# Layer 0 attention of a two-layer kernel: a small total moves to another PSUM bank, and the raw contexts' loads move to another queue and other buffers

## The chip, the cores and the metric

The kernel runs on one core of a Trainium2 chip. The metric is the device time of one execution in microseconds (us). It has five engines that work side by side, each through its own queue in order: TensorE (PE; its weight loads are shown apart as PEld), VectorE (DVE), ScalarE (ACT), GpSimd (POOL) and SyncE (SP), which here only starts transfers. GpSimd can start transfers too. A transfer is started by an instruction of one of these queues and then runs on the core's 16 DMA engines.

## The reference

Two transformer layers run over 8 x 256 tokens of width 512, and both attend to a context of the same shape. Only layer 0's attention matters here, with the weights of the feed-forward part after it, which are prepared meanwhile, and one input of layer 1's attention:

```python
Q = einsum('bshd,hde->bshe', xh, Wh)       # x after its layer norm, 4 heads of 128
K = einsum('bshd,hde->bshe', kh, Wh)       # k = v = context
V = einsum('bshd,hde->bshe', vh, Wh)
scores = einsum('bshe,bthe->bhst', Q, K) / sqrt(hd)
A = maximum(abs((scores * Dn[None]).sum(axis=0)), 1.0)   # summed over the batch
O = einsum('hst,bthe->bshe', A, V).reshape(b, s, dim)
Y = (O - mu) / sqrt(var + GN_EPS) * gn_gamma + gn_beta
return relu(x @ wg_w) * Y @ wo_w
# the feed-forward part's weights:
scale = 1.0 / clip(mean(abs(w)), EPS)
w_q = clip(round(w * scale), -1.0, 1.0) / scale
```

The weights w1, w2, w3 of the feed-forward part become ternary, so each needs the mean of its absolute values first. Layer 1's attention uses the context as its values and ends each head with a normalisation; the kernel takes the mean of each head of 32 off the raw context beforehand and writes the result to device memory.

## The kernel before

Tokens are cut into 16 tiles of 128 (P); a chunk is 512 tokens (CH), so four chunks hold two batch items each. The code of `layer0_attention` is written as loops in Python, but the instructions' order on each queue is not the text's: a planner takes all instructions with their dependencies, an estimated duration for each and the text's order as a priority, and lays them out in time. Each queue then runs in exactly that order, and semaphores hold an instruction until its inputs are there and its buffer is free. Tiles are taken from pools by tag: tiles of one tag share a fixed number of buffers (two in the pool `work` unless said otherwise, one in the PSUM pool `ps`), and a new tile waits until the last use of the buffer's earlier tile is over.

The stage runs as follows.

1. SP loads the residual x, the transposed context `ctxT`, the weights and the decay table `dec`.
2. A loop over the tiles n takes the layer norm (`stats`, `normed`) and transposes it; `queries` (L282) makes one product `pq` for each chunk c and head h, which VectorE copies to a tile q of tag "wy" (L286); `scores` (L289) multiplies q with the context and sums over all chunks in four PSUM tiles. Sixteen pairs (c, h) follow each other. From n = 6 on, each step also calls `ternary.add`: a piece of a weight (up to 768 KB) is loaded by SP into a tile `wst` (L156, two buffers) and ScalarE adds up its absolute values (L166) in `part`.
3. The sums are multiplied with the decay table; Abs and max follow (L323 to L325).
4. A loop over the 16 tiles i: `attended` (L340) makes the output `po` with the values, its layer norm y on VectorE and ScalarE (L71 to L78), and two GpSimd passes over y (L354, L355); `centered` (L327) loads a raw context tile (tag "raw"), takes each head's mean on VectorE (L334, L335), subtracts it on GpSimd (L336), sets each head's last column to one (L337) and stores the tile to `vc_d` (L338). `gated` multiplies with the gate's product `pw` (L360, wy), `turned` transposes wy on TensorE into the PSUM tag "t" (line 108 in the profile, a helper) and ScalarE copies it (L365), and `output` multiplies with `wo` (L371, pz) and adds to x (L372). In every odd i the `values` of a later batch item follow: TensorE makes `pv` (PSUM tag "pv"), ScalarE copies it (L255).
5. Each i ends with `ternary.round`: a weight piece is loaded again, scaled by ScalarE (L191), clipped by VectorE (L192), and a step later written as bf16 (L182). Ahead of the first piece of each weight, `scale` (L168) has TensorE add `part` over the partitions into the PSUM tile wtot, which VectorE reads (L173) and turns into the weight's scale.

`centered` depends on nothing else of the stage, so the planner places it well ahead of its place in the text.

Of the kernel before, what the change touches and what calls it, by code (L numbers as in the profile page):

```python
# [19 lines left out]
F32 = mybir.dt.float32  # L20
# [10 lines left out]
P = 128  # L31
D = 512
KD = D // P
# [4 lines left out]
CH = 512  # L38
NCH = T // CH
H0 = 4  # L40
# [91 lines left out]
class TernaryWeights:  # L132
# [34 lines left out]

    def scale(self, n):  # L168
        nc, g = self.g.nc, self.g
        tot = self.ps.tile([P, KD], F32, tag="t", name="wtot", bufs=1)  # L170
        nc.tensor.matmul(tot, lhsT=g.ones[:, :P], rhs=self.part[:, n], start=True, stop=True)
        mean = g.small.tile([P, 1], F32, tag="wmean", name="wmean")
        nc.vector.tensor_reduce(mean, tot, AX.X, ALU.add)  # L173
        nc.vector.tensor_scalar(mean, mean, 1.0 / (D * FF), 1e-5, ALU.mult, ALU.max)
        nc.vector.reciprocal(self.sc[n], mean)
        nc.vector.reciprocal(g.iw[:, n : n + 1], self.sc[n])
# [19 lines left out]
def layer0_attention(g, tc, cp, qpool):  # L196


    nc = g.nc
# [4 lines left out]
    with ExitStack() as ctx:  # L204
        wp = ctx.enter_context(tc.tile_pool(name="a0w", bufs=1, reuse_waits="tile"))
        work = ctx.enter_context(tc.tile_pool(name="a0work", bufs=2, reuse_waits="tile"))
# [6 lines left out]
        for c in range(NCH):  # L213
            for i in range(c * CH // P, (c + 1) * CH // P):
                nc.sync.dma_start(out=g.X[i], in_=g.x[i * P : (i + 1) * P, :])
            nc.sync.dma_start(
                out=g.ctxT[c],
                in_=g.ctxT_d[:, c * CH : (c + 1) * CH].rearrange("(k p) t -> p k t", p=P),
# [49 lines left out]
        def stats(i):  # L268
            mv = g.small.tile([P, 2], F32, tag="mv", name="mv")
            norm_stats(g, mv, g.X[i])  # L270
            sd = g.small.tile([P, 1], F32, tag="sd", name="sd")
            nc.scalar.activation(sd, mv[:, 1:2], AF.Sqrt, bias=g.eps["ln"])
            return mv, sd
# [8 lines left out]
        def queries(c, h):  # L282
            pq = ps.tile([P, CH], F32, tag="pq", name="pq", bufs=2)
            nc.tensor.matmul(pq, lhsT=G[:, h, :], rhs=xnT[c][:, h, :], start=True, stop=True)
            q = work.tile([P, CH], F32, tag="wy", name="q")
            nc.vector.tensor_copy(q, pq)  # L286
            return q

# [9 lines left out]
        of, q = {0: stats(0)}, {}  # L298
        for n in range(NT + H0 + 1):
            if n + 1 < NT:  # L300
                of[n + 1] = stats(n + 1)
            if n < NT:
                normed(n, *of.pop(n))
            if 0 <= n - H0 < NT:
                q[n - H0] = queries(*divmod(n - H0, H0))
            if 0 <= n - H0 - 1:
                scores(*divmod(n - H0 - 1, H0), q.pop(n - H0 - 1))
            if n < 4:
                values(*divmod(n, 2))
            elif n >= 6:  # L310
                ternary.add()
# [15 lines left out]
        def centered(i):  # L327


            raw = work.tile([P, D], F32, tag="raw", name="raw")  # L330
            nc.sync.dma_start(out=raw, in_=g.ctx[i * P : (i + 1) * P, :])
            by_head = raw.rearrange("p (h d) -> p h d", d=HD1)
            mean = g.small.tile([P, H1], F32, tag="mean", name="mean")
            nc.vector.tensor_reduce(mean, by_head, AX.X, ALU.add)  # L334
            nc.vector.tensor_scalar(mean, mean, 1.0 / HD1, None, ALU.mult)  # L335
            nc.gpsimd.tensor_sub(by_head, by_head, mean.unsqueeze(2).to_broadcast([P, H1, HD1]))  # L336
            nc.gpsimd.memset(by_head[:, :, HD1 - 1 :], 1.0)  # L337
            nc.gpsimd.dma_start(out=g.vc_d[i * P : (i + 1) * P, :], in_=raw)  # L338
# [37 lines left out]
        wy = {}  # L376
        for i in range(NT + 1):
            if i < NT:
                y = attended(i)
                centered(i)  # L380
            if i:
                wyT = turned(wy.pop(i - 1))
            if i < NT:
                wy[i] = gated(pw, y)
            if i + 1 < NT:
                pw = gate(i + 1)
            if i:
                output(i - 1, wyT)
            if NT - 2 <= i < NT:
                g.begun.append(ffn_turned(g, *ffn_input(g, work, i - NT + 2)))  # L390
            if i % 2 and i // 2 + 2 < B:
                for j in range(2):
                    values(i // 2 + 2, j)
            ternary.round()
# [280 lines left out]
def layer1_attention(g, tc, gates):  # L675
    nc = g.nc
    with ExitStack() as ctx:
# [19 lines left out]
        with tc.tile_pool(name="a1ps2", bufs=1, space=PSUM, reuse_waits="tile") as ps, tc.tile_pool(name="a1work", bufs=2, reuse_waits="tile") as work:  # L697
# [112 lines left out]
            def attended(b, hid, rs):  # L810

                nc.gpsimd.tensor_mul(flat(hid), flat(hid), rs.unsqueeze(2).to_broadcast(shape))  # L812
                for j in range(2):
                    i = 2 * b + j
                    hj = hid[:, j, :, :HD1]
                    x, scale = (t.rearrange("p (h d) -> p h d", d=HD1) for t in (g.X[i], lns))
                    nc.gpsimd.tensor_mul(hj, hj, scale)
                    nc.gpsimd.tensor_add(x, x, hj)
# [704 lines left out]
```

## Time and profile before

| what | us |
|---|---|
| median of 3 runs | 1121.75 |
| lowest and highest of them | 1116.63, 1122.53 |
| the profiled execution's own time | 1119.75 |
| its span in the profile | 1118.0 |
| first raw load issued (SP) | 27.5 |
| last raw store issued (GpSimd) | 144.0 |
| last output product pz begins | 242.4 |

The profile comes from one execution. Its rows give a start, a duration, the engine, the line in the kernel, and the operation as output<-inputs; a bracket at the end gives the time that the engine had stood idle before it, and the instruction or transfer whose end released it. In tables of waits the columns are the total, the number of times and the longest. The name of an engine with a q (SPq, POOLq) is its queue, where transfers are started. A wait for several things is put down to the one that came last.

### The profile page before, as it was taken

The page shows a single profiled execution, that of the slowest core. Times are in us where ns is not written, and L with a number is a line of the kernel's source. Part 1 is how long each engine was busy: PE and PEld are TensorE (multiplying, and loading weights), DVE is VectorE, ACT ScalarE, POOL GpSimd, SP SyncE. Part 2 cuts the span into 40 slices and gives each one's busy share as a digit, 9 for nine tenths or more (in the row PEclk, how much of TensorE's full clock was granted, in tenths as well). Part 3 has the DMA queues.
Part 4 walks back from the last instruction along what each step waited for, and adds up shares of the span by engine and source line. Part 5 has one row for each costly group of instructions (what it writes and reads, how often), then busy time and mean ns, then how long its engine had stood idle before and what let it go on. Part 6 is the DMA issues. An engine that isn't in the chain of part 4 may idle for free.

```text
span 1118.0 us, 14714 instructions
## 1 busy us (share of the span) xinstructions
PE 1018.8 (91%) x5207; PEld 614.9 (55%) x5222; DVE 540.5 (48%) x1443; ACT 411.8 (37%) x701; POOL 374.6 (34%) x347
## 2 busy tenths in 40 slices
PE   6979699988899958899889899999999999999994
PEld 5745465543344435555544344555666666777782
DVE  6545445468888755998872883121222111222120
ACT  4345245135576636578752101111212222211211
POOL 0134432230000100254562204454444555544422
PEclk9989899999999989899999999999999999999997
DMA  9676331012233211212012326786777878889982
GB/s 341 249 263 210 128 118 47 1 38 54 54 62 63 44 48 43 67 61 75 24 56 104 93 107 189 172 209 180 205 198 182 215 217 220 223 225 242 236 200 36
DMA packets 100483, 153.65 MB, mean 137 GB/s; under 512 B 38600, under 2 KB 41288, under 8 KB 100376
## 3 DMA queue, kind: packets, MB, share of 16 engines
q1 hardware_dynamic: 81488, 106.94, 31.2%
q0 software_dynamic: 18672, 45.58, 18.1%
q8 instruction: 43, 0.70, 0.3%
q14 instruction: 40, 0.33, 0.1%
q10 hardware_dynamic: 240, 0.10, 0.0%
HBM read 111.24 MB, written 33.49 MB: 129 GB/s over the span
## 4 chain that ended last, share of the span: by engine, by line
PE 68%; DVE 9%; DMA 9%; ACT 7%; issue 3%; POOL 2%; SPq 0%; POOLq 0%; DVEq 0%; ACTq 0%
PE po L1272 13%; PE pg L1255 12%; PE pu L1255 12%; PE p L556 4%; PE pz L371 3%; PE pw L316 3%; PE pt L1312 3%; DMA hqT<-hq 2%; DMA vc_d<-raw 2%; DMA raw<-in_ctx 2%; ACT xe L731 1%; PE pqk L746 1%; PE po L969 1%; DVE ct L754 1%; PE pv L250 1%
## 5 line engine op out<-in xcount | busy, mean ns | idle before, releaser
L1260 DVE TENSOR_TENSOR act<-pu,sg 128x288 f32<-128x288 f32 (+8 forms) x68 | 32.4, 476 | 317.0 <-PE pu L1255 317.0
L1297 POOL DMA_INDIRECT xg<-h_d,tok_of x84 | 81.3, 968 | 205.5 <-DVE of L1307 69.3
L1316 POOL DMA_INDIRECT out_x<-eo,to x84 | 129.8, 1545 | 57.4 <-ACT eo L1354 36.1
L1272 PE MATMUL po<-w,act 128*128 128x512 f32 (+3 forms) x448 | 141.1, 492 | 0.0
L1255 PE MATMUL pg<-xT,w 128*128 128x288 f32 (+7 forms) x512 | 138.4, 413 | 0.8 <-issue 0.8
L1255 PE MATMUL pu<-xT,w 128*128 128x288 f32 (+7 forms) x512 | 136.7, 410 | 0.0
L1354 ACT ACTIVATE eo<-po,slotw 128x512 f32<-128x512 f32 (+3 forms) x112 | 64.2, 578 | 173.2 <-PE po L1272 169.4
L1255 PEld LDWEIGHTS pu<-xT,w 128*128 128x128 f32 x512 | 97.2, 190 | 29.1 <-issue 3.0
L1255 PEld LDWEIGHTS pg<-xT,w 128*128 128x128 f32 x512 | 93.6, 190 | 35.0 <-issue 15.5
L1259 ACT ACTIVATE sg<-pg 128x288 f32<-128x288 f32 (+8 forms) x68 | 28.9, 425 | 213.2 <-PE pg L1255 213.2
L1272 PEld LDWEIGHTS po<-w,act 128*128 128x128 f32 (+3 forms) x448 | 54.4, 161 | 56.1 <-issue 46.3
L556 PE MATMUL p<-wq,xqT 128*128 128x512 bf16 (+1 forms) x379 | 79.5, 361 | 3.1 <-DMA xqT<-xq 2.1
L754 DVE SCALAR_TENSOR_TENSOR ct<-pqk,xe 128x768 f32<-128x768 f32 x64 | 58.3, 950 | 23.7 <-ACT xe L731 11.8
L1313 DVE COPY xT<-pt 128x512 f32<-128x512 f32 (+3 forms) x84 | 51.9, 618 | 20.7 <-PE pt L1312 20.7
L316 PE MATMUL pw<-wg,xnT 128*128 128x512 f32 x128 | 61.1, 623 | 0.0
L556 PEld LDWEIGHTS <-xqT 128*128 128x128 bf16 x384 | 36.7, 98 | 44.2 <-DMA xqT<-xq 6.4
L371 PE MATMUL pz<-wo,wyT 128*128 128x512 f32 x128 | 57.9, 595 | 3.0 <-ACT wyT L365 3.0
L731 ACT ACTIVATE xe<-pd 128x512 f32<-128x512 f32 x96 | 53.9, 598 | 4.7 <-PE pd L727 4.3
L1312 PEld LDWEIGHTS pt<-ident,xg 128*128 128x128 f32 (+4 forms) x336 | 38.9, 140 | 24.4 <-PE po L1272 11.1
L100 DVE BATCH_NORM_STATS2 st<-x 128x6 f32<-128x512 f32 x64 | 43.8, 685 | 12.3 <-DMA x<-in_x 6.0
L812 POOL TENSOR_TENSOR hid<-hid,rsq 128x1024 f32<-128x1024 f32 x8 | 15.3, 1913 | 102.2 <-PE pqk L750 76.3
L575 PE MATMUL py<-wq,hqT 128*128 128x512 bf16 x168 | 41.2, 380 | 8.1 <-DMA hqT<-hq 7.6
(287 smaller groups left out, 1676.3 us busy)
## 6 DMA issues: line engine op xcount, KB each, us to landing
w<-in_w SPq DMA_DIRECT2D x32, 1024.0 KB
w<-in_w SPq DMA_DIRECT2D x32, 512.0 KB
wst<-in_w1T SPq DMA_DIRECT2D x8, 704.0 KB
wst<-in_w3T SPq DMA_DIRECT2D x8, 704.0 KB
wst<-in_w2T SPq DMA_DIRECT2D x6, 768.0 KB
x<-in_x SPq DMA_DIRECT2D x16, 256.0 KB
ctxT<-in_ctxT_d SPq DMA_DIRECT2D x4, 1024.0 KB
raw<-in_ctx SPq DMA_DIRECT2D x16, 256.0 KB
```

The lines of the kernel that those rows point to most:

```text
L316: nc.tensor.matmul(pw, lhsT=xnT[c][:, k, o : o + P], rhs=wg[:, k, :], start=k == 0, stop=k == KD - 1)
L371: nc.tensor.matmul(pz, lhsT=wyT[:, k, :], rhs=wo[:, k, :], start=k == 0, stop=k == KD - 1)
L556: nc.tensor.matmul(pp[:, : z - a], lhsT=xqT[:, k, :], rhs=w[:, k, a:z], start=k == 0, stop=k == KD - 1)
L731: nc.scalar.activation(out, pd, AF.Exp)
L754: nc.vector.scalar_tensor_tensor(ct[:, r : r + 2, :], pqk[:, :, : S + P], 1.0 / math.sqrt(HD1), xe[:, r : r + 2, :], ALU.mult, ALU.mult,)
L1255: nc.tensor.matmul(pp[:, :n], lhsT=w[:, k, cols], rhs=xT[:, k, :n], start=k == 0, stop=k == KD - 1)
L1272: nc.tensor.matmul(po[h * n : (h + 1) * n, :cols], lhsT=act[:, m, j * P : j * P + n], rhs=w[:, m, h * cols : (h + 1) * cols], start=m == 0 ...
L1297: nc.gpsimd.indirect_dma_start(out=xg[:n], out_offset=None, in_=h_d, in_offset=bass.IndirectOffsetOnAxis(ap=g.tok_of[:n, r, j : j + 1], ax ...
L1312: nc.tensor.transpose(pt[:, k, :n], xg[:n, k * P : (k + 1) * P], g.ident[:n, :n])
L1313: nc.vector.tensor_copy(xT, pt[:, :, :n])
L1316: return nc.gpsimd.indirect_dma_start(out=g.out, out_offset=bass.IndirectOffsetOnAxis(ap=rows, axis=0), in_=eo, in_offset=None, compute_op ...
L1354: nc.scalar.activation(eo[:n, at : at + cols], po, AF.Copy, scale=w[r][:n, j : j + 1])
```

## The change

Three lines change. The total wtot of the weights' sums takes a buffer of the PSUM tag "pv" (one bank, that of the values) instead of one of tag "t" (one bank, that of the transposes). The queries of the last chunk's heads 2 and 3 take buffers of tag "raw" instead of "wy". The raw contexts are loaded by GpSimd's queue instead of SP's. As raw tiles and these two queries now share two buffers, the first raw tiles can be loaded only when the last scores have read those queries. The number of buffers, the data and all arithmetic stay.

```diff
     def scale(self, n):
         nc, g = self.g.nc, self.g
-        tot = self.ps.tile([P, KD], F32, tag="t", name="wtot", bufs=1)
+        tot = self.ps.tile([P, D], F32, tag="pv", name="wtot", bufs=1)[:, :KD]
...
             pq = ps.tile([P, CH], F32, tag="pq", name="pq", bufs=2)
             nc.tensor.matmul(pq, lhsT=G[:, h, :], rhs=xnT[c][:, h, :], start=True, stop=True)
-            q = work.tile([P, CH], F32, tag="wy", name="q")
+
+            last = c == NCH - 1 and h >= H0 - 2
+            q = work.tile([P, CH], F32, tag="raw" if last else "wy", name="q")
             nc.vector.tensor_copy(q, pq)
...
             raw = work.tile([P, D], F32, tag="raw", name="raw")
-            nc.sync.dma_start(out=raw, in_=g.ctx[i * P : (i + 1) * P, :])
+            nc.gpsimd.dma_start(out=raw, in_=g.ctx[i * P : (i + 1) * P, :])
```

## The prediction

> **What bounds the kernel now.** I read the page first (which engine fills the span), then the busy time by stretch (where that engine is not full), then the waits of the stage that the change touches, then the order of instructions on each queue around the longest waits.
>
> ```profile
> span 1118.0 us, 14714 instructions
> PE 1018.8 (91%) x5207; PEld 614.9 (55%) x5222; DVE 540.5 (48%) x1443; ACT 411.8 (37%) x701; POOL 374.6 (34%) x347
> ```
>
> TensorE fills 91% of the span, so a saving counts only where TensorE stands idle. The stretches of layer 0 attention show where (columns: stretch, its length, busy time of each engine with instruction counts, granted TensorE clock, share of DMA, GB/s):
>
> ```profile
> 58.00:63.00 5.00, 3.18 (x15) 2.17 (x14) 2.78 (x6) 2.33 (x4) 1.60 (x3) 1.00 0.93 296
> 63.00:80.00 17.00, 11.98 (x57) 7.84 (x57) 7.46 (x18) 8.65 (x14) 6.55 (x10) 0.92 0.70 238
> 80.00:147.00 67.00, 55.77 (x226) 33.34 (x225) 33.89 (x75) 28.45 (x34) 32.83 (x43) 0.89 0.55 185
> 147.00:187.00 40.00, 40.00 (x178) 24.70 (x178) 20.91 (x40) 15.86 (x20) 10.71 (x8) 1.00 0.22 70
> ```
>
> From 147 us on TensorE is full at full clock: by then the last raw context has been centered (last load issued at 134.5 us, last store at 144.0). Before 147 it loses time, and these waits name the losers (58 to 247 us):
>
> ```profile
> PE pt L108 <- DVE wmean L173: 8.2, 1, 8.2
> PE pt L108 <- DVE wmean L174: 5.0, 1, 5.0
> PE pz L371 <- ACT wyT L365: 3.0, 3, 1.7
> PE pt L108 <- DVE wy L360: 2.1, 3, 1.1
> PE s L293 <- DVE q L286: 1.8, 1, 1.8
> PE pv L250 <- ACT v L255: 0.4, 1, 0.4
> ```
>
> Together 20.5 us; 2.5 of them lie after 235 us, at the stage's end, where the change has no part. So 18.0 us of waits remain, and behind the two long ones the next two gate tiles run slowly: 5.41 and 5.31 us where such eight matmuls take 3.60 at full clock, 1.8 + 1.7 = 3.5 us. In all 21.5 us, under 2% of the run, can be had here.
>
> Now the longest wait, TensorE's lines and then VectorE's of the same moment:
>
> ```profile
> 125.74 0.39 PE L351 MATMUL po<-v,dec 128*128 128x128 f32 x2
> 134.28 1.11 PE L108 MATMUL pt<-ident,wy 128*128 128x128 f32 x4 [8.15 <-DVE wmean L173]
> 135.19 5.31 PE L316 MATMUL pw<-wg,xnT 128*128 128x512 f32 x8
> ```
> ```profile
> 129.09 0.69 DVE L360 SCALAR_TENSOR_TENSOR wy<-pw,y 128x512 f32<-128x512 f32 x1 [3.63 <-POOL y L355]
> 129.69 0.68 DVE L334 TENSOR_REDUCE mean<-raw 128x16 f32<-128x512 f32 x1
> ...
> 132.67 0.69 DVE L334 TENSOR_REDUCE mean<-raw 128x16 f32<-128x512 f32 x1 [2.09 <-DMA raw<-in_ctx]
> 133.39 0.17 DVE L335 TENSOR_SCALAR mean<-mean 128x16 f32<-128x16 f32 x1
> 133.47 0.68 DVE L372 TENSOR_TENSOR x<-pz,x 128x512 f32<-128x512 f32 x1
> 134.08 0.15 DVE L173 TENSOR_REDUCE wmean<-wtot 128x1 f32<-128x4 f32 x1
> ```
>
> The transposes' input wy was ready at 129.78 (129.09 + 0.69); their PSUM bank was not, because wtot lay in it and its reader L173 stood in VectorE's queue behind a mean that waited for a raw context. So the chain is: store of a raw tile lands late, its buffer's next load starts late, VectorE's in-order queue holds on L334, and everything behind it (wtot's reader, bn_stats, the new queries) is late.
>
> **The change, part by part** (against the profiled execution, 1119.75 us with a span of 1118.0; it lies 2.0 us under the median of the three runs, 1121.75, from which I forecast).
>
> *The total's bank.* No instruction is added or removed. The transposes (tag t) no longer wait for L173/L174. At the first wait this is worth nothing: wy L360 ends at 78.72 + 0.69 = 79.41, the transposes start at 79.47. At the second they could start at 129.8 instead of 134.28, 4.5 us; if ScalarE's order stayed, the copy wyT (136.98, behind a ScalarE activation that waits for the same VectorE queue) would still hold the output matmuls to 137.6 instead of 140.3, which leaves 2.7. At most the whole stall with its slow clock goes: 8.15 + 1.71 = 9.9. Bounds 2.7 and 9.9. I take 7.9: all but one VectorE wait for a raw context of mean size, 17.5 us / 9 = 1.94 us (the row of L334 on the raw load), which stays exposed. The new wait, values (L250) for the total's reader, I cost at nothing: totals run at 72, 124 and 175 us, the next values' matmuls at 89, 144 and 184, nine us later at the least; without that cover it would cost what the bank costs now.
>
> *The last two queries in raw's buffers.* The first raw load can now start only when a query buffer is released, after the scores at about 61 us, instead of at 27.5. The 1.8 us wait of the scores (query copy L286 at 59.80, behind mean L334 that waited 2.91 us for its load) must go: no mean can be in front of a query any more. Saved: 1.8. What moves: in the trace five raw tiles were centered before the first y (POOL 48 to 72 us). Five loads, five stores, five times 0.69 + 0.17 us on VectorE and 1.05 + 0.12 on POOL go past the query copies, past the table's Abs/max work and into the loop over tiles, on VectorE's and POOL's queues. VectorE is half busy there (33.9 of 67 us), POOL too; so the work fits, but its waits come along. Three iterations that held a pair of raw tiles without the 8 us stall lost 0.42 + 0.54 + 1.66 + 0.46 = 3.1 us, 1.0 each; five tiles are 2.5 iterations more: +2.5 (bounds 0, and 2.5 x 3.4 = 8.5, with 3.4 us what an iteration from 79 to 147 us exceeds the later ones by: transposes at 79.5 and 147.4 us span three iterations with values and two without, 67.9 us, where later ones take 10.9 and 9.1, 50.9 in all; 17 over 5).
> Five loads of 256 KB and about four stores also leave the stretch up to 72 us, where DMA is 70 to 93% busy; 2.3 MB at its 238 to 296 GB/s are 8 to 10 us of transfer. The weights' pieces (ScalarE waited 1.2 to 3.5 us for each) land sooner. This bears on the 5 us wait: po was done at 69.0, but its bn_stats came at 70.48 (behind a mean) and its sd only at 74.63 on ScalarE, behind an Abs that waited 2.64 us for its piece. From there: y 75.14, POOL 76.1 to 78.7, wy 79.4. Bounds: 0, or all 5.0 + 1.8. I take 2.0, one typical piece wait less; the first raw store and load still collide with these pieces.
>
> *The loads on POOL's queue.* SP loses 16 issues of 0.33 us and their waits for stores, 42.3 us in all:
>
> ```profile
> SPq L331 <- DMA vc_d<-raw: 42.3, 12, 8.2
> ```
>
> Behind them only weight pieces were queued, which ScalarE mostly had to release anyway; worth nothing more than the 2.0 above. POOL gains 16 issues. Nearest rows are its own direct transfers of the same size, 562 ns an issue (9 us in all, beside its 72.5 us of waiting for y), and for landing:
>
> ```profile
> L338 POOL DMA_DIRECT2D vc_d<-raw x16: 557/562/774, 49.9 to 144.0; - x16
> DMA to landing us min/median/max: 2.3/4.5/6.5
> ```
> ```profile
> lns<-in_ln_scale POOLq DMA_DIRECT2D x1, 256.0 KB, 3.4
> ```
>
> A rule speaks against this part. The sixteen POOL issues differ by 0.22 us at most although VectorE worked half the time. The Trainium skill ("SBUF — State Buffer", the "DVE blocks DMA" trap) says that a transfer issued by GpSimd stands still while VectorE runs in a mode that takes both ports, about 3.1 us instead of 0.62, and to use the other queues. By the rule 16 loads are late by 2.5 us each, 40 us of lateness, and as much of it exposed as in the trace (18.0 us of TensorE waits to 17.5 us of L334's waits) would make the change slower by over 25 us. By the row it is at most 0.2 us a load, 3 us, hidden. I follow the row, the same queue beside the same VectorE work.
>
> The new wait: a load waits on POOL for the store that empties its buffer, 4.5 us after issue. Queued behind it are y's multiply and add (L354, L355), for which wy and then the transposes wait. In the trace two stores are followed at once by y (2.6 us). If the loads come after y, only 4.5 - 2.6 = 1.9 us of wait is left, with nothing urgent behind it: cost 0. If they come before, y is late by up to 4.5 us against a slack of 1.9 (wy done 154.6, transposes 156.5) to 3.4 us (173.3, 176.7). I take 0, as y is ready when the stores have been issued; the other end is the second rival.
>
> Sum: -7.9 - 1.8 - 2.0 + 2.5 + 0 = -9.2 us: 1110.6 for the profiled execution, 1112.5 from the median. The next thing to be late is VectorE's mean behind its load, at about 1 us an iteration.
>
> **The rivals.** *First, nothing to measure.* Only the bank's certain part (2.7) and the query wait (1.8) come, and 2.5 goes back: -2.0, 1119.8. For it: L334 still waits for loads on an in-order queue, now in 16 cases in the loop, and the order of all queues is planned anew; against it: the 8 us stall needs the shared bank. *Second, slower: POOL's queue becomes the wait.* Loads stand ahead of y in all eight iterations that take a pair: each makes y late by 4.5 + 0.56 - 2.5 (middle of the slack) = 2.6 us; 8 x 2.6 = 20.6, less the sum's 9.2: +11.4, 1133. It decides from four such iterations (4 x 2.6 > 9.2). For it: y has the tightest path of the loop. Against: POOL waited 72.5 us for y's input, so a load can be placed in that gap. *Third, all of it:* with the means off the queries' way every stall before 147 goes, -21.5: 1100.
>
> **How the numbers follow.** Likeliest case 0.50 (1100 to 1116, third included), nothing to measure 0.23, slower 0.27. About 0.5%, 5.6 us, can be told from no change: faster below 1116.1, slower above 1127.4. Range 1099 to 1130: down to the full recovery, up into the slower rival, of which about half (loads ahead of y in seven or eight iterations) is left out. The likeliest case alone: 1100 to 1116.
>
> **What would show it.** Right: no wait of pt for wmean; no wait of s for q; first raw load after 60 us on POOL's queue; busy TensorE in 80 to 147 us above 60 of 67. Wrong: POOL y L354 or its neighbours waiting for the store vc_d, pt waiting for wy by 2 us or more in many iterations, POOL loads taking far over 3.4 us to land, or a TensorE wait for raw work that runs on past 165 us. A layer 0 stage that ends earlier with no earlier end of the run would refute the claim that a saving here passes through.

## The result

The change made the kernel slower. Over 20 runs of each on the same chip the medians are 1117.26 us before and 1123.43 us after; the ratio of the times is 1.0039, with a 95% interval of 1.0022 to 1.0057. That is 2.5 to 6.4 us more, about 4.4, where 9.2 less had been forecast. The three runs shown before the prediction (1121.75) lay on the high side of this kernel's own spread.

The profiled execution of the changed kernel has the same span as that of the kernel before, 1118.0 us, so one profile of each shows no difference at the end. The stage does. Line numbers are two higher from the queries on: L333 is the raw load, L336/L337 the mean, L338 the subtraction, L340 the store, L356/L357 the passes over y, L362 wy, L367 wyT, L373 the output product. First the page's head, then the busy time by stretch (stretch, length, busy time of PE, PEld, DVE, ACT and POOL with counts, granted clock, DMA share, GB/s).

```profile
span 1118.0 us, 14715 instructions
PE 1027.3 (92%) x5222; PEld 617.5 (55%) x5222; DVE 542.7 (49%) x1443; ACT 412.6 (37%) x701; POOL 385.2 (34%) x363
```
```profile
58.00:63.00 5.00, 5.00 (x23) 3.38 (x22) 1.84 (x4) 3.70 (x7) 1.34 (x2) 1.00 0.74 229
63.00:80.00 17.00, 11.58 (x53) 7.45 (x52) 7.82 (x23) 7.63 (x13) 9.94 (x15) 0.87 0.83 280
80.00:147.00 67.00, 56.00 (x209) 32.59 (x207) 33.78 (x68) 24.52 (x29) 39.51 (x54) 0.88 0.50 168
```

TensorE is now full from 58 to 63 us, where it waited for a query before. From 63 to 147 nothing is better: 67.6 us busy of 84 after, 67.8 before (62.7 and 69.9 in the second profiles further down), and the clock is 0.87 and 0.88 where it was 0.92 and 0.89. The waits of TensorE in the stage (total, times, longest):

```profile
PE pt L108 <- DVE wy L362: 7.2, 4, 3.0
PE pt L108 <- DVE wmean L174: 5.4, 1, 5.4
PE pv L250 <- ACT v L255: 3.6, 2, 3.3
PE pz L373 <- ACT wyT L367: 2.5, 4, 0.7
```

The 8.2 us wait for wmean's L173 and the 1.8 us for q are gone. In their place the transposes wait for wy itself. (The 5.4 us against L174 is such a wait too: L174 ends at 76.52, but wy, which the transposes need and which stands just in front of it, ends at 76.46.) What is new on GpSimd's and VectorE's queues, and VectorE's row of before (L334) last:

```profile
POOL raw L333 <- DMA vc_d<-raw: 16.5, 7, 5.7
```
```profile
DVE mean L336 <- DMA raw<-in_ctx: 26.8, 10, 7.7
```
```profile
DVE mean L334 <- DMA raw<-in_ctx: 17.5, 9, 3.6
```

GpSimd stands 16.5 us on loads whose buffer is still being stored, and VectorE's wait for raw tiles grew from 17.5 to 26.8 us. GpSimd's order of time shows what stands behind such a load:

```profile
80.93 1.28 POOL L356 TENSOR_TENSOR y<-y,gam 128x512 f32<-128x512 f32 x1
83.97 0.56 POOL L333 DMA_DIRECT2D raw<-in_ctx  x1 [1.77 <-DMA vc_d<-raw]
84.55 1.28 POOL L357 TENSOR_TENSOR y<-y,bet 128x512 f32<-128x512 f32 x1
...
106.63 0.54 POOL L333 DMA_DIRECT2D raw<-in_ctx  x1
112.83 0.54 POOL L333 DMA_DIRECT2D raw<-in_ctx  x1 [5.66 <-DMA vc_d<-raw]
115.03 1.04 POOL L338 TENSOR_TENSOR raw<-raw,mean 128x512 f32<-128x512 f32 x1 [1.66 <-DVE mean L337]
116.13 0.13 POOL L339 MEMSET raw<- 128x16 f32 x1
116.55 0.56 POOL L340 DMA_DIRECT2D vc_d<-raw  x1 [0.30 <-POOL raw L339]
117.13 1.27 POOL L356 TENSOR_TENSOR y<-y,gam 128x512 f32<-128x512 f32 x1
```

At 83.97 a load is placed between the two passes over one y (y 1, counted by iterations). At 106.63 the planner put a pair of loads and the work of a raw tile ahead of y 3, whose first pass came at 117.13. GpSimd's queue alone does not explain that: y 3's input was written only at 116.19. VectorE shows why, with the longest of its waits:

```profile
106.23 0.17 DVE L101 BATCH_NORM_AGGREGATE mv<-st 128x2 f32<-128x6 f32 x1
114.05 0.69 DVE L336 TENSOR_REDUCE mean<-raw 128x16 f32<-128x512 f32 x1 [7.65 <-DMA raw<-in_ctx]
114.65 0.17 DVE L73 BATCH_NORM_AGGREGATE mv<-st 128x2 f32<-128x6 f32 x1
...
115.38 0.81 DVE L78 TENSOR_SCALAR y<-po,mv,rs 128x512 f32<-128x512 f32 x1
```

The load of 106.63 took 7.4 us to land, the longest of the sixteen:

```profile
DMA to landing us min/median/max: 2.8/3.5/7.4
```

It ran beside two weight pieces that SP had started at 105.03 (DMA 0.91 busy from 106 to 112 us), and y's own statistics (L73) stood behind its mean. So VectorE's queue held y 3 up for 7.6 us, GpSimd's for another 0.9 (116.19 to 117.13).

The landmark in all that follows is the start of the last output product, the stage's end on TensorE: 242.38 us before, 244.10 after. The same two programs profiled once more give the measure of chance:

> The kernel before, profiled a second time. If the stage's end is set by the order of the queues and not by chance, the last product begins within 1 us of 242.4; the later stages may differ by several us with the granted clock.

> The changed kernel, profiled a second time: last product within 1 us of 244.1 by the same theory. If the 3 us that its first profile lost between 242 and 692 us are chance of the clock, this profile shows another figure there; if they belong to the change, again 2 to 4 us more than before.

The last product's line, of the kernel before again and of the changed kernel again:

```profile
238.71 3.70 PE L371 MATMUL pz<-wo,wyT 128*128 128x512 f32 x8 [0.68 <-ACT wyT L365]
```
```profile
247.71 3.70 PE L373 MATMUL pz<-wo,wyT 128*128 128x512 f32 x8 [0.68 <-ACT wyT L367]
```

The expected 1 us was too narrow: the stage's end moves by 3.6 to 3.7 us between executions of one program. Means are 240.5 before and 245.9 after, 5.4 us later. In the second profile of the changed kernel the longest wait of VectorE stands at the same place, in front of y 3's statistics:

```profile
117.17 0.69 DVE L336 TENSOR_REDUCE mean<-raw 128x16 f32<-128x512 f32 x1 [9.03 <-DMA raw<-in_ctx]
```

### The profile page after: what moved, and what is told of

The parts are those of the page before. It is cut to its first block, busy times and chain, and to the rows that moved or that the text cites. A ratio compares the mean times of both kernels' runs of the same rounds, so it can differ in the third digit from the quotient of the medians.

```text
span 1118.0 us, 14715 instructions
## 1 busy us (share of the span) xinstructions
PE 1027.3 (92%) x5222; PEld 617.5 (55%) x5222; DVE 542.7 (49%) x1443; ACT 412.6 (37%) x701; POOL 385.2 (34%) x363
## 4 chain that ended last, share of the span: by engine, by line
PE 68%; DVE 10%; DMA 8%; ACT 7%; POOL 4%; issue 3%; SPq 0%; POOLq 0%; DVEq 0%; ACTq 0%
PE po L1274 13%; PE pg L1257 12%; PE pu L1257 12%; PE p L558 3%; PE pz L373 3%; PE pt L1314 3%; DMA raw<-in_ctx 3%; PE pw L318 2%; DMA hqT<-hq 2%; ACT xe L733 1%; PE pqk L748 1%; PE s L295 1%; PE pq L284 1%; DMA vc_d<-raw 1%; PE po L971 1%
## 5 line engine op out<-in xcount | busy, mean ns | idle before, releaser
L318 PE MATMUL pw<-wg,xnT 128*128 128x512 f32 x128 | 63.6, 643 | 0.0
L373 PE MATMUL pz<-wo,wyT 128*128 128x512 f32 x128 | 58.1, 597 | 2.6 <-ACT wyT L367 2.5
```

Of the source, the lines that this page charges most:

```text
L318: nc.tensor.matmul(pw, lhsT=xnT[c][:, k, o : o + P], rhs=wg[:, k, :], start=k == 0, stop=k == KD - 1)
L373: nc.tensor.matmul(pz, lhsT=wyT[:, k, :], rhs=wo[:, k, :], start=k == 0, stop=k == KD - 1)
```

## The experiments

All edits are to the kernel before unless another is named; "time" is the ratio to the kernel before, with its interval.

| kernel | last product, us | median, us | time |
|---|---|---|---|
| before (two profiles) | 242.4, 238.7 | 1117.26 | 1 |
| bank alone | 237.7 | 1119.24 | 0.998 (0.9957 to 1.0003) |
| queries alone | 237.5 | 1120.83 | 0.9999 (0.9982 to 1.0015) |
| queue alone | 254.0 | 1133.84 | 1.012 (1.0083 to 1.0157) |
| bank + queries | 236.7 | 1119.12 | 0.998 (0.9958 to 1.0003) |
| queries + queue | 249.0 | 1125.51 | 1.0046 (1.0026 to 1.0066) |
| all three: the change (two profiles) | 244.1, 247.7 | 1123.43 | 1.0039 (1.0022 to 1.0057) |
| the change, y first | 240.3 | 1118.13 | 0.9978 (0.9954 to 1.0002) |
| the change, no means | 250.0 | not comparable | not comparable |
| spread buffers, SP | 228.3 | 1105.91 | 0.9895 (0.9854 to 0.9937) |
| spread buffers, half of the loads on GpSimd | 227.4 | 1108.30 | 0.9906 (0.987 to 0.9941) |
| spread buffers, GpSimd | 229.4 | 1108.49 | 0.9895 (0.9861 to 0.9928) |
| spread buffers, GpSimd, 8 stores too | 230.2 | 1106.03 | 0.9881 (0.984 to 0.9922) |

The groups were run against their own runs of the kernel before (medians 1117.26 to 1121.31), so kernels of different groups are compared by the ratios, not by the medians.

**The three parts one by one.** The diffs are the three hunks of the change, each alone, and the first two together.

> Only the total's PSUM bank is changed. The measure is the start of the last output product pz in the profile (242.4 us before, 244.1 after the whole change) beside the time. If the bank matters as the prediction's first step had it: the 8.2 us wait of the transposes shrinks to 2 to 5 us, the last product begins at 235 to 240, the time falls by 3 to 7 us. If VectorE's late queue was the real cause and the bank only where it showed: the transposes wait for wy or for a later step instead, the last product begins at 241 to 243, the time moves by less than 2 us.

> Only the last two queries take raw's buffers; the loads stay on SP. Theory POOL (the loads on POOL's queue make y late): this part alone gains the 3 us that the scores' end gained in the whole change, last product at 238 to 241. Theory CROWD (all sixteen raw tiles now fall into the loop, whichever queue loads them): the last product at 244 to 250, as late as after the whole change or later, since the shared bank is still there; the time 2 to 8 us up.

> Only the loads' queue is changed; two raw tiles are still loaded early. Theory POOL: loads that wait for stores stand before y on POOL; last product at 245 to 252, time 3 to 10 us up. Theory CROWD: POOL's queue is harmless, last product at 241 to 244, time within 2 us.

> Bank and queries changed, loads on SP: the whole change without its third part. Theory POOL: both gains and no price, last product at 233 to 239, time 4 to 9 us under before. Theory CROWD: last product at 243 to 246, time 0 to 4 us over before, like the whole change.

The part that costs is the queue, as theory POOL said: alone 13 us (1.2%), more than the 3 to 10 expected. Queries alone do not crowd the loop; the stage ends 3 us earlier than the mean of the two profiles of before, and CROWD falls. (That is less than two profiles of one kernel differ by, and the time stays at 0.9999.) The gains came at less than half their expected size: bank and queries together take 3.8 us off the stage's mean end, little more than the 3.6 of chance, and 0.2% off the time, with an interval that still touches 1. The reason shows in TensorE's waits of bank + queries: the wait for wmean is gone, but wy takes its place.

```profile
PE pt L108 <- DVE wy L361: 9.8, 4, 3.6
PE pz L372 <- ACT wyT L366: 5.3, 4, 2.5
```

So the shared bank was where the lateness of VectorE's queue showed, not its cause: the second expectation for the bank alone. There too the transposes wait for wy, 5.8 us in four waits, where it was 2.1. The stage's end fits the first expectation (237.7); the time, about 2 us less with an interval that touches 1, decides nothing.

The queue alone is worse than the queue inside the change for a reason of its own. SP's queue had the loads of x and the context in front of the raw tiles; GpSimd's queue had nothing, and the planner put seven raw loads and seven stores between 13 and 60 us. The DMA engines move hardly more there than before (302 GB/s from 13 to 58 us, 294 before), but VectorE stands 13.8 us on raw tiles between 13 and 60 us, where it was 2.9, and the queries' copies stand behind. The stretch from 13 to 58 us and TensorE's wait for q there:

```profile
13.00:58.00 45.00, 34.19 (x169) 25.64 (x169) 27.24 (x72) 13.95 (x31) 15.93 (x26) 0.92 0.80 302
```
```profile
47.10 1.22 PE L293 MATMUL s<-q,ctxT 128*128 128x256 f32 x2 [5.04 <-DVE q L286]
```

34.2 us busy, where it was 44.1. With the queries in raw's buffers the first load has to wait for the scores:

> Queries and queue changed, the bank not. The queue alone ended at 254.0 us, the whole change at 244.1. If the queries' buffers are what keeps GpSimd's loads out of the scores' loop (the extra price of the queue alone): last product at 243 to 248, no wait of the scores for q. If the bank made the difference: 251 or later.

Measured: last product at 249.0, no wait for q. So it is the queries' edit that takes the early collision away (254.0 to 249.0; the ratios, 1.012 and 1.0046, have intervals clear of each other); the figure lies a little over the expected 248. What the bank adds is not shown: 249.0 against 244.1 and 247.7, at nearly the same ratio.

**What on GpSimd's queue costs.** The first kernel moves the loads behind y by an edge in the planner alone; the second leaves VectorE's means out.

```diff
-            nc.gpsimd.dma_start(out=raw, in_=g.ctx[i * P : (i + 1) * P, :])
+            load = nc.gpsimd.dma_start(out=raw, in_=g.ctx[i * P : (i + 1) * P, :])
+            if i >= 2:   # order only: after y of iteration i // 2 - 1
+                tc.add_manual_dep(load.ins, ys[i // 2 - 1].ins.name, ...)
```

> The whole change, with each pair of raw loads put behind the y of the iteration before on GpSimd's queue (order only, nothing waits for new data), so that no load's wait for a store stands in front of a y. Theory P1 (the wait for stores in front of y is the price): the last product, at 244.1 us after the change and 236.7 with bank and queries alone, comes back to 236 to 240, the time 3 to 7 us under the changed kernel. Theory P2 (the price is that the loads are late and VectorE's queue stands on the mean, 26.8 us in the changed kernel): the loads come later still, the last product stays at 243 to 250, VectorE waits 25 us or more for raw.

```diff
-            mean = g.small.tile([P, H1], F32, tag="mean", name="mean")
-            nc.vector.tensor_reduce(mean, by_head, AX.X, ALU.add)
-            nc.vector.tensor_scalar(mean, mean, 1.0 / HD1, None, ALU.mult)
+            mean = g.ones[:, :H1]
```

> The whole change, with the heads' means left out (a tile of ones is subtracted instead), so the result differs; VectorE has no instruction that waits for a raw tile, and GpSimd waits for the load itself. Theory P1: y still stands behind loads that wait for stores, last product at 241 to 245. Theory P2: VectorE's waits of 26.8 us are gone, last product at 230 to 237. About 14 us of VectorE's own work goes with it, but VectorE is half idle there.

With y first, GpSimd's queue runs without one wait for a store:

```profile
82.24 0.56 POOL L346 DMA_DIRECT2D vc_d<-raw  x1 [0.30 <-POOL raw L345]
82.82 1.28 POOL L364 TENSOR_TENSOR y<-y,gam 128x512 f32<-128x512 f32 x1
84.18 1.26 POOL L365 TENSOR_TENSOR y<-y,bet 128x512 f32<-128x512 f32 x1
85.38 1.70 POOL L333 DMA_DIRECT2D raw<-in_ctx  x2
```

The stage ends at 240.3, 5.6 us before the mean of the changed kernel, just past P1's range and outside P2's; the ratios give 0.9978 / 1.0039, about 7 us less. So the place of the loads ahead of y is most of what the change paid for (the stage ends 3.6 us later than with bank and queries alone, no more than chance). Which queue passed the price on it does not show, since VectorE's wait for raw fell too, where P2 had expected it to stay:

```profile
DVE mean L342 <- DMA raw<-in_ctx: 20.2, 9, 5.9
```

Without means the last product comes at 250.0, later than both theories said. (The time is not comparable: other values reach layer 1's routing, and the program's conditional last part runs too.) VectorE waits for no raw tile, and the stage is late all the same, so waits on GpSimd's queue are enough to make it late. But P2's wait has moved there and not gone, since GpSimd now waits for the load itself too:

```profile
POOL raw L333 <- DMA vc_d<-raw: 14.7, 7, 5.2
POOL raw L336 <- DMA raw<-in_ctx: 12.1, 7, 3.9
```
```profile
DVE wy L360 <- POOL y L355: 72.0, 16, 11.3
```

VectorE waits up to 11.3 us for y, because y's input lies ready for 6.6 to 7.8 us in y 0, 2, 3 and 4 before GpSimd comes to it, behind instructions of the raw chain that wait.

In the changed kernel itself both paths show. The time that y 0 to 5 stand on GpSimd's queue with their input ready (from the end of L78 to the first pass, and between the passes) is 8.4 and 10.3 us in its two profiles, 4.4 with y first, 3.2 with bank and queries alone. VectorE's waits for raw are 26.8 and 29.7 us, with longest waits of 7.7 and 9.0; with bank and queries alone:

```profile
DVE mean L335 <- DMA raw<-in_ctx: 14.4, 11, 3.1
```

From y 2's input to y 3's, where those longest waits lie, 20.1 and 21.4 us pass, 12.0 with bank and queries alone. How the price divides between P1 and P2 is not settled.

**The chain store, load taken apart.** Raw tiles 4 to 15 get buffers that no store has to empty, the normalised queries of chunks that are through with their gates; bank and queries stay changed.

```diff
-            raw = work.tile([P, D], F32, tag="raw", name="raw")
+            if i < 4:
+                raw = work.tile([P, D], F32, tag="raw", name="raw")
+            else:
+                raw = xnT[i // 4 - 1][:, i % 4, :]
```

> Bank and queries changed, loads on SP, and the raw tiles 4 to 15 are loaded into the normalised queries' buffers xnT, a chunk of them once its last gate product is over, so twelve of sixteen loads wait for no store. If the chain store, load, mean is what holds VectorE: VectorE's waits for raw fall from 14.4 to under 6 us, the last product from 236.7 to 227 to 233, the time 6 to 12 us under before. If the waits come from loads in flight with weight pieces: last product at 235 to 238.

> The same buffers with the loads on GpSimd's queue. If GpSimd's queue costs only through the waits for stores (P1 and P2 alike): last product within 2 us of the kernel with these buffers and SP. If the queue itself is slow to land 256 KB or its issue holds y: 4 us later or more.

On SP the last product starts at 228.3 and the time is 0.9895 of before. VectorE's waits for raw, in both kinds of buffer:

```profile
DVE mean L338 <- DMA raw<-in_ctx: 4.1, 2, 3.1
DVE mean L338 <- DMA xnT<-in_ctx: 2.2, 2, 1.2
```

6.3 us instead of 14.4, a little over the "under 6" expected. The stage ends 12 us before the mean of the kernel before, and the time falls by as much, so a saving in this stage does reach the end of the run. On GpSimd's queue the last product starts 1.1 us later, within the 2 us, at the same ratio, but not for nothing: VectorE's waits for raw are twice as long,

```profile
DVE mean L339 <- DMA raw<-in_ctx: 6.9, 2, 5.4
DVE mean L339 <- DMA xnT<-in_ctx: 6.4, 2, 4.9
```

the last product takes 5.40 us instead of 3.70 (the clock is 0.89 from 225 to 240 us, 1.00 on SP), and the shorter end of the program, shown next, takes 4.6 us off again. So with most of the waits for stores gone the queue still costs some 1 to 3 us of the stage by these two profiles, where it cost 7 to 11 in the change. Both versions beat both kernels, by about 1%.

**The program's end.** In the kernels with all sixteen loads on GpSimd the end is shorter (but for the one without means, whose last part starts more transfers). GpSimd's last drain (times min/median/max in ns), before and after:

```profile
L1519 POOLq DRAIN  x3: 46/110/6562, 1110.2 to 1117.7; - x3
```
```profile
L1521 POOLq DRAIN  x3: 46/109/2928, 1114.2 to 1117.7; - x3
```

From the start of GpSimd's last add to the last instruction it is 14.6 us before (1103.39 to 1118.0) and 9.4 after (1108.57 to 1118.0); 3.6 of these 5.2 us are the drain itself, what gives the rest is open. Two runs changed the number of GpSimd's transfers:

```diff
-            nc.sync.dma_start(out=raw, in_=g.ctx[i * P : (i + 1) * P, :])
+            (nc.gpsimd if i % 2 else nc.sync).dma_start(out=raw, in_=g.ctx[i * P : (i + 1) * P, :])
```

> The spread buffers, with every second raw load on GpSimd's queue (8 of 16) and the others on SP's. GpSimd's last drain took 6562 ns in all six profiles with the raw loads on SP and 2928 ns in all six with the sixteen loads on GpSimd. If the drain depends on the number of GpSimd's transfers evenly (227 ns each): 4.7 us here. If it goes by a threshold: 6.56 or 2.93. Last product at 227 to 230 in either case; the time 10 to 15 us under before.

```diff
-                        nc.sync.dma_start(out=g.out[i * P : (i + 1) * P, :], in_=g.X[i])
+                        nc.gpsimd.dma_start(out=g.out[i * P : (i + 1) * P, :], in_=g.X[i])
```

> The spread buffers with all raw loads on GpSimd's queue, and also the first eight stores of the output (between 590 and 620 us) moved from SP's queue to GpSimd's, so 24 more transfers there than before. If the drain falls evenly with each transfer: about 1.1 us, tail of 9 us. If it goes round in steps of a ring: 6 us or more again. If the stores on GpSimd's queue delay other work there, later stages grow by some us.

The drain with 8 loads and with 24 transfers more:

```profile
L1523 POOLq DRAIN  x3: 46/109/7175, 1095.3 to 1103.1; - x3
```
```profile
L1524 POOLq DRAIN  x3: 46/109/3541, 1099.4 to 1103.5; - x3
```

Neither an even fall nor two fixed values: 6562, 7175, 2928 and 3541 ns for 0, 8, 16 and 24 transfers more. It rises by 613 ns for 8 transfers, twice, and if it goes on rising so it drops by 4.86 us (7175 + 613 - 2928) somewhere between 8 and 16, as something that goes round would do. Whether anything goes round, and what, was not tried. (The kernel without means, with sixteen such loads and its own last part, drains for 5667 ns, so the count over the whole program is what would have to be followed.)

## Why the prediction was wrong

**The step that failed** is the new wait on GpSimd's queue, which the sum took at 0 "as y is ready when the stores have been issued". The planner, which lays out by its own estimates, put raw loads ahead of a y or between its two passes in six iterations (y 0 to 5). From bank + queries to the whole change the stage's end goes from 236.7 to 244.1 and 247.7, 7 to 11 us instead of 0. Part of that is the wait that the step speaks of: y stands on GpSimd's queue with its input ready for 8.4 and 10.3 us instead of 3.2. Part of it comes by a path that the prediction had put at about 1 us an iteration, VectorE's mean behind its load: one load landed after 7.4 and 8.8 us, where 3.4 had been taken, and held VectorE up for 7.7 and 9.0 us in front of y 3. How the 7 to 11 us divide is open. The second rival, which the forecast gave 0.27, had the place of the loads and its deciding point (four iterations); its 2.6 us an iteration, all of them on GpSimd's queue, were too many: both paths together come to 1.2 to 1.8.

The queue's price alone, 9.2 us on the means, would only have used up the 9.2 us that had been forecast as saved; for a stage that ends later the gains had to fail as well.

**The gains were over-sized.** The bank was taken at 7.9 us with the stall's slow clock; alone it is worth 2.8 us on the stage's mean end (237.7 to 240.5), near the lower bound of 2.7 and within what two profiles of one kernel differ by. The wait had belonged to VectorE's late queue, and wy, on that queue too, came next. Part of it was chance: the 8.15 us stall of the profile shown was 6.9 in the second one. The query wait was right: it is gone, and the first gate product starts at 60.27 and 60.10 instead of 63.48 and 61.41, 2.3 us on the means for the 1.8 predicted. The 2.0 us for weight pieces that land sooner did not come: the first transposes wait 5.4 us, where it was 5.0, and y 0 itself stands behind a load that waits 2.55 us for its store.

**What held.** GpSimd's loads took the row's price in issue and median: 541 to 770 ns an issue, 3.5 us to land, for 0.56 and 3.4 expected; only the slowest landing, 7.4 us, is far over it, a sign of being wrong that the prediction had named. Busy TensorE above 60 of 67 us, a sign of being right, did not come (56.0).

```profile
L333 POOL DMA_DIRECT2D raw<-in_ctx x16: 541/542/770, 59.4 to 141.5; - x16
```

The rule of the Trainium skill ("SBUF — State Buffer", the "DVE blocks DMA" trap) would, by the prediction's estimate from it, have had them late by 2.5 us each. The issues differ by 0.23 us at most, and while the slowest load was under way VectorE stood idle (106.4 to 114.05 us), so that load was late for another reason. Whether VectorE worked in such a mode beside any load the traces do not show. The moved tiles' +2.5 was not measured by itself.

**Where the saving or loss went at the end.** Mean of the two profiles each: the stage's end 5.4 us later; from there to the last add 2.1 us longer (861.0 and 864.8 before, 864.5 and 865.6 after); the program's end 5.0 us shorter. Sum +2.5, which is what these four executions differ by (1119.75 and 1119.58 to 1119.81 and 1124.56), at the low end of the measured 2.5 to 6.4. The prediction had no term for the end at all; without the shorter end the change would have cost about 5 us more. The 2.1 us are not settled: TensorE's order is the same outside the stage, only the granted clock differs there, by as much between two executions of one kernel as between the kernels.

## What to carry to other kernels

A transfer costs its queue more than its issue: it costs whatever it waits for, and everything behind it waits along, as it does on the queue of the engine that reads what is loaded. So put a load that must wait for a buffer on a queue where nothing urgent stands behind it, or give it a buffer that is free. Moving a wait's visible victim (here the transposes' bank) gains little while the queue that made it late stays as it is; look for what that queue waits on. And before relying on one profile for a change of half a per cent, profile the same program twice.

## What the runs showed of the hardware

The spread between executions of one program goes with TensorE's granted clock: over the 20 runs of the changed kernel time and mean clock correlate with -0.87, 0.72 us for each 0.001 (1116.91 us at 0.973, 1127.36 at 0.964), and with -0.82 to -0.92 in the five other kernels with 20 or more runs. Which of the two drives the other is not shown. And the last drain of GpSimd took the same number of nanoseconds in all six profiles of kernels with raw loads on SP (6562), and the same again in six of the seven with sixteen loads on GpSimd (2928; the seventh is the one without means), a difference of 3.6 us for transfers that were over some 970 us earlier.
